# Row fetches on two helper queues, PSUM copies on VectorE, and the steps behind a pair's sums spread over six pairs

## The chip, the core and the metric

The kernel runs on one core of a Trainium2 chip. The metric is the device time of one execution in microseconds. Ten runs of the kernel before had a median of 15896.23 us (15894.68 to 15897.35).

An engine runs its own instructions in order and waits on semaphores for the others: TensorE (PE) multiplies matrices, VectorE (DVE) and ScalarE (ACT) work on elements, GpSimd (POOL) here issues gathers, SyncE (SP) issues transfers. ScalarE issues transfers too.

## The reference

One layer of a graph network with 50,000 nodes of 160 features (64 scalars and 32 vectors of three) and 1,650,000 edges, sorted by destination. Each edge takes the features of its source, mixes them with its four attributes and five small weight matrices into a message, and the messages of a destination are summed. The sum goes through two more matrices, and the result is `layernorm(x + (x + relu(h)))`.

```
ss, vv = (s[src], v[src])
e0 = sh[:, 0:1]
e1 = sh[:, 1:4]
dot = jnp.einsum('eui,ei->eu', vv, e1)
out0 = C0 * (ss * e0 @ W1 + dot * INV3 @ W2)
...
m_agg = jax.ops.segment_sum(m, dst, num_segments=n)
hs = m_agg[:, :MUL0] @ Ws * LIN_S
...
return x + jax.nn.relu(h)
...
x = _layernorm(x + _L0_gnn_ref(...), axis=-1)
```

## The kernel before

The weights commute with the sums, so the kernel first sums `attribute k times source row` over the edges of a destination, for k = 0 to 3, and applies one combined 160x(4x160) matrix afterwards (`weights` builds it as BWa and BWb).

The edges are cut into units of 128. Six units (G) are a group, whose destinations fit into a window of 32 nodes (W). Two groups are a pair (PG), four a chunk (QG), and 20 a superblock (SG) of 120 units. There are 12,894 units, 2,149 groups, 1,075 pairs, 538 chunks, 108 superblocks and 391 blocks of 128 nodes.

`load` brings a superblock's source and destination numbers (`ri`) and attributes (`ra`) with three SyncE transfers, casts the numbers on ScalarE (`rf`, line 203), makes byte offsets of rows of x from them (`ro`, line 206), and transposes everything on PE, so that an edge stands on a partition. `place` subtracts the first destination of each group (`rel`).

`group_sums` does a pair. For each unit one indirect DMA on GpSimd gathers 128 rows of x into one of eight `xg` buffers (line 236). VectorE makes a one-hot matrix of the destinations (`hot`, line 241) and multiplies it by the four attributes (`ha`, line 244). PE multiplies each unit's `ha` with its rows into `ps` (line 249), and ScalarE copies `ps` to `A` (line 255).

One unit in 60 is not gathered by GpSimd. Its rows are fetched by SyncE: `HELP` names pairs 4 and 9 of each superblock, and the last unit of such a pair is a helper unit, with a buffer `xr`. `fetch` works in four batches of 32 rows, one after each of the four pairs before: a TENSOR_LOAD brings 32 offsets into registers (line 323), then 32 transfers of one row of 640 B each follow (line 328).

When a chunk's two pairs are summed, `second` runs after the next pair's sums: `apply_weights` transposes `A` on PE into `pt` (line 267), ScalarE copies it to `at` (270), PE multiplies by BWa and BWb into `phc` (277), ScalarE copies to `hp` (281). For each node block that is now complete, `block` loads its x rows (`xt`, SyncE, line 289), doubles them on ScalarE (line 291), makes a one-hot matrix (`hot2`, 295), adds the chunks' rows with PE into `phb` (300), and calls `norm`: VectorE's relu and add (`y`, 151) and statistics (153, 155), ScalarE's square root (157), VectorE's reciprocal and scaling (158, 160), and a ScalarE store (161).

The order of instructions on each engine is chosen by a scheduler from this program. Transfers issued by SyncE and ScalarE signal their landing on eight semaphores, taken in turn by both queues together in the built order. A transfer waits, before it is issued, until the transfer eight places earlier, which used the same semaphore, has landed. Gathers on GpSimd have eight semaphores of their own.

Behind the main loop there is a second path (from line 400) for edges that don't fit the windows; it isn't taken here.

Of the kernel before, what the change touches and what calls it, by code (L numbers as in the profile page):

```python
# [30 lines left out]
F32 = mybir.dt.float32  # L31
I32 = mybir.dt.int32
U8 = mybir.dt.uint8
AF = mybir.ActivationFunctionType
ALU = mybir.AluOpType
AX = mybir.AxisListType
ET = mybir.EngineType
PSUM = bass.MemoryType.PSUM

P = 128  # L40
MUL0, MUL1 = 64, 32
D = MUL0 + 3 * MUL1
NK = 4
EPS = 1e-5
C0 = 1.0 / math.sqrt(MUL0 + MUL1)
C1 = math.sqrt(3.0 / (MUL0 + 2 * MUL1))
# [5 lines left out]
W = 32  # L52
# [4 lines left out]
HELP = {ET.SP: (4, 9)}  # L57
# [19 lines left out]
def tile_gnn_resnorm(ctx: ExitStack, tc: tile.TileContext, x, src, dst, attr, W1, W2, W3, W4, W5, Ws, Wv, out, n_edges):  # L77
# [12 lines left out]
    nc.gpsimd.memset(eps_t, EPS)  # L90
# [57 lines left out]
    def norm(pool, ph, x2, n, row):  # L148

        y = pool.tile([P, D], F32, name="y")  # L150
        nc.vector.scalar_tensor_tensor(y[:n], ph, 0.0, x2, op0=ALU.max, op1=ALU.add)  # L151
        st = pool.tile([P, 6], F32, name="st")
        nc.vector.bn_stats(st[:n], y[:n])
        mv = pool.tile([P, 2], F32, name="mv")
        nc.vector.bn_aggr(mv[:n], st[:n])  # L155
        rstd = pool.tile([P, 1], F32, name="rstd")
        nc.scalar.activation(rstd[:n], mv[:n, 1:2], AF.Sqrt, bias=eps_t[:n])  # L157
        nc.vector.reciprocal(rstd[:n], rstd[:n])  # L158
        o = pool.tile([P, D], F32, name="o")
        nc.vector.tensor_scalar(o[:n], y[:n], mv[:n, 0:1], rstd[:n], op0=ALU.subtract, op1=ALU.mult)  # L160
        nc.scalar.dma_start(out[row, :], o[:n])
# [15 lines left out]
    with tc.tile_pool(name="once", bufs=1) as once, tc.tile_pool(name="raw", bufs=2) as rawp, \  # L177
# [3 lines left out]
            tc.tile_pool(name="hp", bufs=alive + 3) as hpp, tc.tile_pool(name="node", bufs=3) as np_, \  # L181
# [8 lines left out]
        nc.vector.tensor_copy(slotsP, slots)  # L190

        def load(s):

            n = (min(NG, (s + 1) * SG) - s * SG) * G
            u0 = s * SG * G
            e = slice(u0 * P, (u0 + n) * P)
            ri = rawp.tile([P, 2, P], I32, name="ri")
            ra = rawp.tile([P, P, NK], F32, name="ra")
            nc.sync.dma_start(ri[:n, 0, :], src1[e].rearrange("(u p) o -> u (p o)", p=P))
            nc.sync.dma_start(ri[:n, 1, :], dst1[e].rearrange("(u p) o -> u (p o)", p=P))  # L200
            nc.sync.dma_start(ra[:n].rearrange("u p k -> u (p k)"), attr[e].rearrange("(u p) k -> u (p k)", p=P))
            rf = rawp.tile([P, 2, P], F32, name="rf")
            nc.scalar.copy(rf[:n], ri[:n])

            ro = rawp.tile([P, P], I32, name="ro")
            nc.scalar.mul(ro[:n], ri[:n, 0, :], 4.0 * D)
            offsets[s] = ro
            pi = psI.tile([P, 2, P], F32, name="pi")
            for i in range(2):
                nc.tensor.transpose(pi[:, i, :n], rf[:n, i, :], ident[:n, :n])  # L210
            si = idxp.tile([P, P], I32, name="si")
            nc.vector.tensor_copy(si[:, :n], pi[:, 0, :n])
            pk = psK.tile([P, NK, P], F32, name="pk")
            for k in range(NK):
                nc.tensor.transpose(pk[:, k, :n], ra[:n, :, k], ident[:n, :n])
            return s, n, si, pi, pk

        def place(loaded):

            s, n, si, pi, pk = loaded  # L220
            rel = idxp.tile([P, P], F32, name="rel")
            nc.vector.tensor_tensor(
                rel[:, :n].rearrange("p (g j) -> p g j", j=G), pi[:, 1, :n].rearrange("p (g j) -> p g j", j=G),
                baseB[:, s * SG:s * SG + n // G].unsqueeze(2).to_broadcast([P, n // G, G]), op=ALU.subtract)
            nc.vector.tensor_reduce(extremes[:, 0, s:s + 1], rel[:, :n], axis=AX.X, op=ALU.min)
            nc.vector.tensor_reduce(extremes[:, 1, s:s + 1], rel[:, :n], axis=AX.X, op=ALU.max)
            return si, rel, pk

        def group_sums(placed, u, ng, q):

            si, rel, pk = placed
            n = ng * G
            xg = rowp.tile([P, PG * G, D], F32, name="xg")
            xr = fetched.pop(q, None)
            for j in range(n - (xr is not None)):
                nc.gpsimd.indirect_dma_start(  # L236
                    out=xg[:, j, :], out_offset=None, in_=x,
                    in_offset=bass.IndirectOffsetOnAxis(ap=si[:, u + j:u + j + 1], axis=0))

# [6 lines left out]
                                    .to_broadcast([P, n, NK, W]), op=ALU.mult)  # L246
            ps = psA.tile([P, PG, D], F32, name="ps")
            for j in range(n):
                nc.tensor.matmul(ps[:, j // G, :], ha[:, j].rearrange("p k w -> p (k w)"),  # L249
                                 xr if xr is not None and j == n - 1 else xg[:, j, :],  # L250
                                 start=j % G == 0, stop=j % G == G - 1)
            for eng in HELP:
                fetch(q, eng)
            A = sump.tile([P, PG, D], F32, name="A")
            nc.scalar.copy(A[:, :ng], ps[:, :ng])  # L255
            return A, ng

        def apply_weights(pairs):
# [3 lines left out]
            for f0, f1 in ((0, P), (P, D)):  # L262
                pt = psM.tile([P, QG, P], F32, name="pt", tag="misc")
                g = 0
                for A, n in pairs:
                    for i in range(n):
                        nc.tensor.transpose(pt[:f1 - f0, g, :], A[:, i, f0:f1], ident)  # L267
                        g += 1
                at = sump.tile([f1 - f0, NK, QG, W], F32, name=f"at{f0}")
                nc.scalar.copy(at[:, :, :ng].rearrange("f k g w -> f g k w"),  # L270
                               pt[:f1 - f0, :ng].rearrange("f g (k w) -> f g k w", w=W))
                parts.append(at)
            ph = psM.tile([P, D], F32, name="phc", tag="misc")
# [7 lines left out]
            nc.scalar.copy(hp[:ng * W], ph[:ng * W])  # L281
            return hp, ng * W

        def block(b, hps):
            nb = min(P, N - b * P)
            cs = of_block[b]
            row = slice(b * P, b * P + nb)
            xt = np_.tile([P, D], F32, name="xt")
            nc.sync.dma_start(xt[:nb], x[row, :])
            x2 = np_.tile([P, D], F32, name="x2")  # L290
            nc.scalar.mul(x2[:nb], xt[:nb], 2.0)  # L291
# [4 lines left out]
                                    rr[:, :len(cs)].unsqueeze(2).to_broadcast([P, len(cs), P]), op=ALU.is_equal)  # L296
            ph = psM.tile([P, D], F32, name="phb", tag="misc")
# [3 lines left out]
            norm(np_, ph[:nb], x2[:nb], nb, row)  # L301
# [3 lines left out]
        offsets, fetched = {}, {}  # L305
        ppair = SG // PG
        steps = P // ROWS
        todo = {}
        for s in range(NSC):
            for eng, at in HELP.items():  # L310
                for m in at:
                    q = s * ppair + m
                    if q >= steps and (s * SG + (m + 1) * PG) <= NG:
                        for i in range(steps):
                            todo.setdefault((q - steps + i, eng), []).append((q, s, (m + 1) * PG * G - 1, i))

        def fetch(q, eng):

            for q1, s, u, i in todo.pop((q, eng), []):
                if i == 0:  # L320
                    fetched[q1] = farp.tile([P, D], F32, name=f"xr{list(HELP).index(eng)}")
                xr = fetched[q1]
# [8 lines left out]
        loaded = {0: load(0)}  # L331
# [16 lines left out]
        placed = {0: place(loaded.pop(0))}  # L348
        hps, pairs, ready = {}, [], []
        c = 0  # L350

        def second(c, pairs):
            hps[c] = apply_weights(pairs)
            for b in after[c]:
                block(b, hps)
            for old in [o for o in hps if o < of_block[min(nblocks - 1, (after[c] or [0])[-1])][0]]:
                del hps[old]

        g = 0
        while g < NG:  # L360
            s = g // SG
            if g % SG == 0 and s + 1 < NSC:
                loaded[s + 1] = load(s + 1)
            ng = min(PG, NG - g, (s + 1) * SG - g)
            got = group_sums(placed[s], (g - s * SG) * G, ng, s * ppair + (g - s * SG) // PG)
            if ready:
                second(*ready.pop())
            pairs.append(got)
            g += ng
            if g % QG == 0 or g == NG:  # L370
                ready.append((c, pairs))
                pairs, c = [], c + 1
            if g % SG == 0 and g < NG:
                placed[s + 1] = place(loaded.pop(s + 1))
                del placed[s]
        second(*ready.pop())


# [85 lines left out]
    with tc.tile_pool(name="edges2", bufs=2) as ep, tc.tile_pool(name="ops2", bufs=2) as op, \  # L464
# [3 lines left out]
        with tc.For_i(0, blocks, 1) as b:  # L468
# [51 lines left out]
            nc.scalar.mul(xt, xt, 2.0)  # L520
            norm(np_, ph, xt, NBLK, row)
# [33 lines left out]
```

## Time and profile before

| | before |
|---|---|
| median of 10 runs | 15896.23 us |
| the profiled execution | 15896.43 us |
| its span | 15894.3 us |
| mean granted TensorE clock | 0.676 |
| HBM traffic | 73 GB/s over the span |
| share of the 16 DMA engines' span taken by gathers (q0) | 24.6% |
| share taken by SyncE's transfers (q1) | 2.2% |

A page of the profile has the busy time of each engine, then groups of instructions: line, engine, operation, output and inputs, shape, count, then busy microseconds, mean nanoseconds of one, and the idle time of that engine just before them with what ended it. "issue" there means that the engine waited for nothing that the profile shows. A view by line gives minimum/median/maximum durations in ns. The queue in order of time gives start, length, engine, line, tiles and count, with idle time in brackets. Instructions of SyncE, and those of ScalarE that issue transfers, don't count as busy; they are shown as SPq and ACTq. The profile is even over its whole length: the busy shares of the 40 slices differ by a tenth at most.

### The profile page before, as it was taken

To read this page: it belongs to the slowest core of one execution; us is meant where nothing else is said; L and a number is where in the kernel's file an instruction comes from. 1 tells how busy PE (TensorE), PEld (TensorE's weight loads), DVE (VectorE), ACT (ScalarE), POOL (GpSimd) and SP (SyncE) were. 2 spreads that over 40 slices of the span, in tenths; PEclk is the share of its full clock that TensorE was granted. 3 is DMA by queue.
4 is the path that set the end of the run, shared out by engine and by line. 5 is a ranking of instruction groups with operands and counts; after the bars stand their busy time and mean duration, and the time that the engine had idled before them with its cause. 6 is when DMAs were issued, how large, how long until landed. Compare 5 with 4: busy or idle time off the path is not lost. (4 is left out here: it accounts for less than half of the span.)

```text
span 15894.3 us, 172106 instructions
## 1 busy us (share of the span) xinstructions
PE 8955.7 (56%) x43943; PEld 7311.8 (46%) x43944; DVE 3430.4 (22%) x5361; ACT 1480.1 (9%) x3691; POOL 11990.8 (75%) x12691
## 2 busy tenths in 40 slices
PE   5555565555555655555555555555555555555565
PEld 4444444444444444444444444444444444444454
DVE  2222222222222222222222222222222222222222
ACT  0000000000000000000000000100000000000000
POOL 7777777777777777777777777777777777777776
PEclk7666666666666666666666666666766666666666
DMA  3222222222222222222222222222222222222222
GB/s 76 74 73 74 74 73 74 74 73 74 74 74 73 74 74 73 74 75 73 74 74 75 73 74 74 74 74 74 74 74 74 73 75 74 73 74 74 73 74 69
DMA packets 823370, 1173.58 MB, mean 74 GB/s; under 512 B 250282, under 2 KB 606342, under 8 KB 822244
## 3 DMA queue, kind: packets, MB, share of 16 engines
q0 software_dynamic: 608640, 1039.56, 24.6%
q1 hardware_dynamic: 156868, 90.41, 2.2%
q10 hardware_dynamic: 56864, 32.58, 0.7%
q8 instruction: 350, 5.73, 0.1%
q14 instruction: 648, 5.31, 0.1%
HBM read 1129.30 MB, written 32.25 MB: 73 GB/s over the span
## 5 line engine op out<-in xcount | busy, mean ns | idle before, releaser
L236 POOL DMA_INDIRECT xg<-in_x,si x12680 | 11989.2, 946 | 3870.7 <-issue 3720.4
L249 PE MATMUL ps<-xg,ha 128*128 128x160 f32 x25360 | 5632.5, 365 | 1459.8 <-DMA xg<-in_x,si 1381.9
L249 PEld LDWEIGHTS ps<-xg,ha 128*128 128x128 f32 x25360 | 4348.6, 225 | 2585.2 <-DMA xg<-in_x,si 2303.9
L244 DVE TENSOR_TENSOR ha<-hot,pk 128x1536 f32<-128x1536 f32 x1075 | 1883.3, 1752 | 7937.2 <-PE ps L249 7936.9
L249 PE MATMUL ps<-xr,ha 128*128 128x160 f32 x428 | 186.1, 538 | 5114.6 <-DMA xr<-in_x 3842.4
L249 PEld LDWEIGHTS ps<-xr,ha 128*128 128x128 f32 x428 | 107.7, 312 | 5181.3 <-issue 3001.3
L151 DVE SCALAR_TENSOR_TENSOR y<-phb,x 128x160 f32<-128x160 f32 x391 | 125.1, 320 | 4291.1 <-ACT x L291 4258.7
L267 PE MATMUL pt<-ident,A 128*128 128x128 f32 (+1 forms) x4298 | 866.8, 338 | 266.8 <-DVE y L151 249.2
L277 PE MATMUL phc<-BWa,at 128*128 128x160 f32 x4304 | 939.3, 376 | 17.9 <-ACT at L270 14.4
L277 PEld LDWEIGHTS phc<-BWa,at 128*128 128x128 f32 x4304 | 832.5, 249 | 87.6 <-ACT at L270 69.5
L277 PE MATMUL phc<-BWb,at 32*128 32x160 f32 x4304 | 846.8, 342 | 0.0
L300 PE MATMUL phb<-hp,hot 128*128 128x160 f32 x4584 | 805.0, 331 | 7.3 <-ACT hp L281 7.3
L270 ACT COPY at<-pt 128x512 f32<-128x512 f32 (+1 forms) x1076 | 607.3, 579 | 1947.9 <-PE pt L267 1937.7
L277 PEld LDWEIGHTS phc<-BWb,at 32*128 32x128 f32 x4304 | 701.7, 213 | 119.5 <-issue 119.3
L267 PEld LDWEIGHTS pt<-ident,A 128*128 128x128 f32 (+1 forms) x4298 | 567.3, 146 | 410.8 <-DVE y L151 311.4
L300 PEld LDWEIGHTS phb<-hp,hot 128*128 128x128 f32 x4584 | 723.2, 211 | 61.4 <-issue 48.2
L255 ACT COPY A<-ps 128x320 f32<-128x320 f32 x1075 | 445.6, 425 | 3245.0 <-PE ps L249 3159.3
L241 DVE TENSOR_TENSOR hot<-slotsP,rel 128x384 f32<-128x384 f32 x1075 | 594.2, 553 | 30.5
L291 ACT ACTIVATE x<-xt 128x160 f32<-128x160 f32 x391 | 131.4, 336 | 4875.3 <-DMA xt<-in_x 4873.2
L295 DVE TENSOR_TENSOR hot<-slotsP,rr 128x768 f32<-128x768 f32 (+2 forms) x391 | 362.2, 926 | 4.4 <-PE phb L300 4.4
L281 ACT COPY hp<-phc 128x160 f32<-128x160 f32 x538 | 157.4, 293 | 1780.9 <-PE phc L277 1750.6
L157 ACT ACTIVATE rstd<-mv,eps_t 128x1 f32<-128x1 f32 x391 | 115.2, 295 | 1763.7 <-DVE mv L155 1759.5
(70 smaller groups left out, 1003.2 us busy)
## 6 DMA issues: line engine op xcount, KB each, us to landing
xr<-in_x SPq DMA_DIRECT2D x27392, 0.6 KB
xg<-in_x,si POOLq DMA_INDIRECT x12680
xt<-in_x SPq DMA_DIRECT2D x390, 80.0 KB
out<-o ACTq DMA_DIRECT2D x390, 80.0 KB
ra<-in_attr SPq DMA_DIRECT2D x107, 240.0 KB
ri<-in_src SPq DMA_DIRECT2D x107, 60.0 KB
ri<-in_dst SPq DMA_DIRECT2D x107, 60.0 KB
baseI<-base_d SPq DMA_DIRECT2D x1, 1076.0 KB
```

What stands on the lines that cost most here:

```text
L236: nc.gpsimd.indirect_dma_start(out=xg[:, j, :], out_offset=None, in_=x, in_offset=bass.IndirectOffsetOnAxis(ap=si[:, u + j:u + j + 1], axi ...
L241: nc.vector.tensor_tensor(hot[:, :n], slotsP[:, 0:W].unsqueeze(1).to_broadcast([P, n, W]), rel[:, u:u + n].unsqueeze(2).to_broadcast([P, n ...
L244: nc.vector.tensor_tensor(ha[:, :n], hot[:, :n].unsqueeze(2).to_broadcast([P, n, NK, W]), pk[:, :, u:u + n].rearrange("p k u -> p u k").un ...
L249: nc.tensor.matmul(ps[:, j // G, :], ha[:, j].rearrange("p k w -> p (k w)"), xr if xr is not None and j == n - 1 else xg[:, j, :], start=j ...
L255: nc.scalar.copy(A[:, :ng], ps[:, :ng])
L267: nc.tensor.transpose(pt[:f1 - f0, g, :], A[:, i, f0:f1], ident)
L270: nc.scalar.copy(at[:, :, :ng].rearrange("f k g w -> f g k w"), pt[:f1 - f0, :ng].rearrange("f g (k w) -> f g k w", w=W))
L277: nc.tensor.matmul(ph[:ng * W], at[:, k, :ng].rearrange("f g w -> f (g w)"), bw[:, k, :], start=i == 0, stop=i == 2 * NK - 1)
L281: nc.scalar.copy(hp[:ng * W], ph[:ng * W])
L291: nc.scalar.mul(x2[:nb], xt[:nb], 2.0)
L295: nc.vector.tensor_tensor(hot2[:, :len(cs)], slotsP.unsqueeze(1).to_broadcast([P, len(cs), P]), rr[:, :len(cs)].unsqueeze(2).to_broadcast( ...
L300: nc.tensor.matmul(ph[:nb], hot2[:r, i, :nb], hp[:r], start=i == 0, stop=i == len(cs) - 1)
```

## The change

- `HELP` now has periods: SyncE fetches one unit in 44 and ScalarE one in 48, in batches of 32 rows that are spread evenly over the period. The last batch is issued two pairs ahead of the pair that uses the rows. SyncE has the buffers `xr0`, ScalarE `xr1`, three of each. Helper units become 292 for SyncE and 267 for ScalarE (before: 214 for SyncE alone).
- The copies out of PSUM to `A`, `at` and `hp` go from ScalarE to VectorE.
- The combined weights and epsilon are scaled so that half of the sum is normalized: `y = relu(h)/2 + x` with epsilon/4. The doubling of x on ScalarE goes away.
- The steps behind a pair's sums become functions that a table runs after later pairs: the cast of a loaded superblock after the first pair, its transposes after the fourth; `ha` of a pair before the sums of the pair in front; `turn` one pair after the chunk, the weights and the block's loads after two, the block's sums after four, the square root after five, the store after six.
- `hp` and `node` pools get one more buffer.

```
-HELP = {ET.SP: (4, 9)}
+HELP = {ET.SP: 44, ET.Activation: 48}
...
             A = sump.tile([P, PG, D], F32, name="A")
-            nc.scalar.copy(A[:, :ng], ps[:, :ng])
+            nc.vector.tensor_copy(A[:, :ng], ps[:, :ng])
...
             hp = hpp.tile([P, D], F32, name="hp")
-            nc.scalar.copy(hp[:ng * W], ph[:ng * W])
+            nc.vector.tensor_copy(hp[:ng * W], ph[:ng * W])
...
+        for h, (eng, period) in enumerate(HELP.items()):
+            first = PG * G + h * period // 2
+            while True:
+                at = [int(first + i * period / nbatch) // (PG * G) for i in range(nbatch)]
+                q = at[-1] + 2
+                if q >= len(pairs) or pairs[q][2] < PG:
+                    break
+                s, g, ng = pairs[q]
+                u = (g - s * SG + ng) * G - 1 - len(helped.get(q, []))
+                helped.setdefault(q, []).insert(0, (eng, h))
+                for i, p in enumerate(at):
+                    batches.setdefault(p, []).append((eng, h, q, s, u, i))
+                first += period
...
+        def fetch(p):
+            for eng, h, q, s, u, i in batches.get(p, []):
                 if i == 0:
+                    fetched[q, h] = farp.tile([P, D], F32, name=f"xr{h}")
+                xr = fetched[q, h]
...
+        for p, (s, g, ng) in enumerate(pairs):
+            if p % per == 0 and s + 1 < NSC:
+                raws[s + 1] = load(s + 1)
+                after_pair(p + 1, do_cast, s + 1)
+                after_pair(p + 4, do_place, s + 1)
+            rows = gather(placed[s], (g - s * SG) * G, ng * G,
+                          [fetched.pop((p, h)) for _, h in helped.get(p, [])])
+            if p + 1 < len(pairs):
+                s1, g1, ng1 = pairs[p + 1]
+                has[p + 1] = spread(placed[s1], (g1 - s1 * SG) * G, ng1 * G)
+            sums.append(group_sums(rows, has.pop(p)))
+            fetch(p)
+            if (g + ng) % QG == 0 or g + ng == NG:
+                after_pair(p + 1, do_turn, c, sums)
+                for b in after[c]:
+                    after_pair(p + 4, do_block, b)
+                    after_pair(p + 5, do_root, b)
+                    after_pair(p + 6, do_store, b)
+                after_pair(p + 2, do_weights, c)
+                sums, c = [], c + 1
+            for f, args in later.pop(p, []):
+                f(*args)
```

`spread` is the part of `group_sums` that made `hot` and `ha`; `gather` the part with the indirect DMAs; `turn` the transposes of `apply_weights`; `nodes` the loads and one-hot matrix of `block`; `norm1`, `norm2` and `norm3` the three parts of `norm` up to the statistics, the square root, and the rest with the store. Their instructions are otherwise those shown above.

## The prediction

> **What bounds the kernel now.** I read the busy times first, then the costliest groups, then the GpSimd queue in order of time, then the queue of SyncE. All of these are views of the one profiled execution of before.
>
> ```profile
> PE 8955.7 (56%) x43943; PEld 7311.8 (46%) x43944; DVE 3430.4 (22%) x5361; ACT 1480.1 (9%) x3691; POOL 11990.8 (75%) x12691
> L236 POOL DMA_INDIRECT xg<-in_x,si x12680 | 11989.2, 946 | 3870.7 <-issue 3720.4
> L249 PE MATMUL ps<-xr,ha 128*128 128x160 f32 x428 | 186.1, 538 | 5114.6 <-DMA xr<-in_x 3842.4
> ```
>
> GpSimd looks 75% busy, but nearly all of its idle time (3720.4 of 3870.7 us) ended by itself ("issue"). The queue in order of time shows why: a gather starts every 1.25 us, whatever the other engines do.
>
> ```profile
> 8022.07 0.94 POOL L236 DMA_INDIRECT xg<-in_x,si  x1 [0.30 <-issue]
> 8023.32 0.95 POOL L236 DMA_INDIRECT xg<-in_x,si  x1 [0.30 <-issue]
> 8024.57 0.94 POOL L236 DMA_INDIRECT xg<-in_x,si  x1 [0.31 <-issue]
> ```
>
> The view of line 236 has the first start at 7.0 and the last at 15861.1 us, so the spacing is 15854.1/12,679 = 1.2504 us. Gathers fill the span: 7 us of start, 12,679 x 1.2504, and 33 us from the start of the last one. The profiled execution took 15896.43 us (its span 15894.3 and 2.1 around it), 0.2 above the median. PE waits 3842 us for helper rows (xr), yet GpSimd loses nothing by it, because eight xg buffers let it run ahead.
>
> The next lines are SyncE's and ScalarE's issue: one row of a helper unit, the load of 32 row offsets, the store, a run of helper rows, one xt, and what SyncE waited for.
>
> ```profile
> L328 SPq DMA_DIRECT2D xr<-in_x x27392: 227/228/403, 20.5 to 15837.8; - x200
> L323 SPq TENSOR_LOAD <-ro x856: 2083/2178/2443, 18.2 to 15825.1; - x172
> L161 ACTq DMA_DIRECT2D out<-o x391: 338/338/371, 179.1 to 15885.6; - x196
> ...
> 7999.88 7.65 SPq L328 DMA_DIRECT2D xr<-in_x  x24
> ...
> 8024.70 0.37 SPq L289 DMA_DIRECT2D xt<-in_x  x1
> ...
> SPq L328 <- DMA out<-o: 4483.5, 385, 67.5
> ```
>
> Twenty-four rows in 7.65 us: (7.65 - 0.228)/23 = 0.3227 us a row. The 4483.5 us tell that SyncE can be held by a store of ScalarE. All DMAs of SyncE and ScalarE take eight completion semaphores in turn, and each waits until the DMA eight places earlier has landed. Today the eight are nearly all SyncE's own.
>
> **The change, part by part.** *Gathers removed.* 292 units go to SyncE and 267 to ScalarE, 559 in place of 214, so 12,335 gathers are left of 12,680. GpSimd alone would give 7.0 + 12,334 x 1.2504 + 33.2 = 15,463, with 2 around it 15,465 us: 431 less. That is 14.35 us for each of the 1,075 pairs, and the price of any cover from here on.
>
> *SyncE's added work.* 292 units are 1,168 batches: 2.24 us for the offsets (2.18 and the step to the next instruction) and 32 x 0.3227, so 12.57 us, 14,682 in all. 390 xt at 0.43 (the row's 0.37 and the step) make 168; 321 loads of edges at about 0.45 (0.41 to 0.52 apart in the trace) 144. Sum 14,994 us against 15,424 of gathers: it fits only if a batch loses no more than 0.37 us.
>
> *What a batch loses.* In the built program the two helpers stand alternately: of SyncE's 37,376 rows, 30,116 have just four of SyncE's own DMAs among the last eight (24,285 of 27,392 had eight of eight before), and SyncE waits on semaphores 0, 2, 4, 6 while ScalarE waits on 1, 3, 5, 7. So a row waits for the row four back to land. The trace has the landing, as the last update of that semaphore: 1.414 us after the issue starts on average (26,994 rows; 5 to 95% 1.183 to 1.658), and a held row starts 0.017 later. Four issues take 4 x 0.3227 = 1.29. With eight places the landing was hidden (2.58); with four the mean of the longer of both is 1.445, 0.361 a row. The added wait isn't in the trace of before; I bound it by its rows. Low end 0 (a quarter of the landings are under 1.285). High end: the first row of a batch lands after 1.333, those in full flow after about 1.42, so one queue at work adds 0.09; a second queue may add as much again, 1.505 + 0.017, mean 0.386 a row: 30,116 x 0.064 = 1,917. I take half of that addition, 0.371 a row: 30,116 x 0.0486 = 1,464 us, since the row is nearer to the measured mean than to either end.
>
> *ScalarE's queue.* It loses the copies (445.6 + 607.3 + 157.4 busy) and x2 (131.4), and gains 1,068 batches at 12.57, 13,425 us; with 29,980 rows at the four-back wait (1,457), 391 roots (115), stores (391 x 0.40 = 156) and 108 casts (78) it comes to 15,231, some 1,230 below SyncE's 16,458: 3.1 us of slack for each root. Each root now stands in front of a batch and waits for VectorE's mv, which waits for PE. In the built order 140 of 363 roots come at most one SyncE batch behind the last rows that PE must first consume; for these, a round of PE (8955.7/1,075 = 8.3 us a pair) and 0.9 of VectorE can be exposed. 151 such roots in all x (9.2 - 3.1) = 920 us at most, 0 at least (PE's round mostly over); I take 460, as half of a round is likely done. Behind the root stand 32 rows and the store; SyncE meets them through the shared semaphores.
>
> *Moved to VectorE.* Nearest rows are its operations out of PSUM: 128x160 0.320 us (line 151), 128x384 0.553 (line 241), so 128x320 0.49, 128x512 0.69: 1,075 x 0.49 + 1,076 x 0.69 + 538 x 0.32 = 1,441 us. VectorE goes to 4,870 us, 4.5 a pair, beside a batch of 12.57; PE's 8.3 a pair hides there as well. If that cover were gone the 1,441 would count in full.
>
> *Spread over six pairs, halved weights, earlier hot2, ha and place.* No matmul or transpose is added, and x2 goes because the weights carry the half. These steps are moved on PE and VectorE, which wait for rows either way: nothing, and the reach of 0 to -131 (x2) lies beside the helper queues. The xt load is moved among SyncE's rows; it landed within 2.01 us (issued 8007.63, used 8009.64), and the next offsets load of 2.24 mostly covers it. Without that, 390 x 0.7 = 273.
>
> Sum: SyncE 14,994 + 1,464 + 460, and some 80 for the first offsets (18) and the two pairs and the tail after the last rows: 16,998, with 2 around it 17,000 us. GpSimd then waits for xg buffers, since PE stands at xr.
>
> **A rule against the change.** ScalarE's stores overlap 75 times with a helper row on SyncE, and in 73 both keep their 338 and 228 ns (the others 457, and 595 with 403), so I price no collision between the two issuers. The Trainium skill, Perfetto Trace Analysis, section DMA Instruction — HWDGE (DVE, Sync), says that the two share one descriptor generator, locked while an instruction uses it. If the whole 228 ns were locked, 71,552 rows would need 16,314 us, slower than before by that alone; the overlaps say that the lock is far shorter.
>
> **Rivals.** *The lanes don't bind* (faster, 15,465 us): the four-back wait costs under 0.37 us a batch, GpSimd keeps its 1.25 us spacing, and the change gives its 431 us. For it: a quarter of the landings come in time, SyncE's bare work fits. Against: the mean landing is beyond 1.29, and SyncE is at 97% without any wait. *ScalarE's in-order waits decide* (18,930): all 391 roots expose the round, 391 x 6.1 = 2,385 in place of 460. For it: today's 4483.5 us of SyncE behind stores; against: 223 of 363 roots have two batches or more to spare. *VectorE's copies hold GpSimd up* (16,900): 15,465 + 1,441, if each copy stopped the gathers for its length. Against: gathers run from 942 to 1143 ns, median 946, beside 3430 us of VectorE. *The helpers don't take what they should*: 559 units are in the built program, so this is out.
>
> **How the numbers follow.** The lane-limited case 0.60, its own range 16,130 (landings as measured, no exposed root: 14,994 + 1,057 + 80) to 18,190 (14,994 + 1,917 + 920 + 273 + 80, rounded); lanes not binding 0.20; the roots 0.11; VectorE 0.05; a balance within 0.2% (15,864 to 15,928) 0.04. A measurement of this kernel can tell 0.2%. Faster 0.20, same 0.04, slower 0.76. The range must reach the rival on the other side, 15,460, and ends at 18,200.
>
> **What would show it.** Right: GpSimd's idle time goes from "issue" to PE's ps; starts of rows on both queues 0.36 to 0.38 us apart inside a batch, with each fourth held; SyncE without any long rest; PE idle at xr. Wrong: gathers still 1.25 us apart to the end, or rows still 0.3227 apart (the window isn't what holds them), or the long waits all before roots (then the third case).

## The result and the profile after

The changed kernel took 19441.55 us (median of 8 runs, 19427.64 to 19459.75) against 15896.37 for the kernel before: a ratio of 1.223 (95% interval 1.222 to 1.224). The prediction had the side right and the size wrong: 17,000 us, with a range that ended at 18,200. The profiled execution has a span of 19463.3 us.

The page of the changed kernel, its engines and the groups that answer to those shown of before (busy time and mean, then the idle time before them and what ended most of it):

```profile
PE 7548.6 (39%) x43943; PEld 6895.9 (35%) x43944; DVE 4672.6 (24%) x8050; ACT 185.6 (1%) x611; POOL 11663.5 (60%) x12346
L246 POOL DMA_INDIRECT xg<-in_x,si x12335 | 11661.9, 945 | 7662.3 <-issue 3677.4
L267 PE MATMUL ps<-xr,ha 128*128 128x160 f32 x1118 | 373.5, 427 | 9070.7 <-DMA xr<-in_x 8231.3
L152 DVE SCALAR_TENSOR_TENSOR y<-phb,xt 128x160 f32<-128x160 f32 x391 | 126.4, 323 | 8887.0 <-DMA xt<-in_x 8883.5
```

GpSimd's own pauses ("issue", 0.30 us a gather) are as before, and when nothing holds it a gather still starts every 1.25 us. New are 3,985 us in which it waits for others, nearly all of it in these two waits (in total, times, longest):

```profile
POOL xg L246 <- DVE rel L235: 2747.9, 97, 42.8
POOL xg L246 <- PE ps L267: 1067.8, 272, 19.8
```

PE stands 9,071 us at helper rows. VectorE stands 8,884 us at `xt`, a tile that SyncE loads between its rows. In the kernel before, ScalarE stood at `xt` and VectorE behind it, and the gathers kept their pace all the same:

```profile
L151 DVE SCALAR_TENSOR_TENSOR y<-phb,x 128x160 f32<-128x160 f32 x391 | 125.1, 320 | 4291.1 <-ACT x L291 4258.7
L291 ACT ACTIVATE x<-xt 128x160 f32<-128x160 f32 x391 | 131.4, 336 | 4875.3 <-DMA xt<-in_x 4873.2
```

So such a wait alone tells little; what does is that GpSimd is now held. The kernel no longer runs at the pace of the gathers, but at that of the two helper queues, as the path below shows.

SyncE's queue in order of time, where 24 rows took 7.65 us before:

```profile
1016.06 12.37 SPq L362 DMA_DIRECT2D xr<-in_x  x30
1028.80 0.37 SPq L313 DMA_DIRECT2D xt<-in_x  x1
1031.50 11.19 SPq L362 DMA_DIRECT2D xr<-in_x  x30
```

Thirty rows in 12.37 us are 0.419 us a row. Over the whole trace the mean step inside a batch is 0.420 on SyncE and 0.417 on ScalarE. The same microseconds on the other engines, lines left out between:

```profile
1025.81 5.97 ACTq L362 DMA_DIRECT2D xr<-in_x  x15
...
1030.13 0.87 PE L267 MATMUL ps<-xr,ha 128*128 128x160 f32 x2 [44.16 <-DMA xr<-in_x]
...
1030.60 0.33 DVE L152 SCALAR_TENSOR_TENSOR y<-phb,xt 128x160 f32<-128x160 f32 x1 [42.46 <-DMA xt<-in_x]
...
1032.27 0.29 ACT L161 ACTIVATE rstd<-mv,eps_t 128x1 f32<-128x1 f32 x1 [68.30 <-DVE mv L156]
...
1034.62 1.14 ACTq L362 DMA_DIRECT2D xr<-in_x  x3
...
1039.74 0.35 DVE L167 TENSOR_SCALAR o<-y,mv,rstd 128x160 f32<-128x160 f32 x1
...
1040.13 0.38 ACTq L168 DMA_DIRECT2D out<-o  x1
1040.61 2.27 ACTq L362 DMA_DIRECT2D xr<-in_x  x5
```

This is a ring. SyncE's last rows and `xt` (1028.80) let PE and VectorE go on after 44 and 42 us of standing. VectorE makes `y`, then in its own order the copies and `ha` that had piled up, and only at 1039.74 `o`. ScalarE issued its last row at about 1035.5, and then stood until 1040.13 for the store of that `o`; its next rows, for which PE will stand again, could only follow behind.

To see how much of the time is ring and how much is rows, I followed the path back from an instruction of PE near the end: each instruction to that of its dependencies which ended last, by the semaphores of the built program and the starts, ends and landings of the trace. "Rows" are issues, landings and offset loads of both queues. Of the changed kernel, e1 and f1 the first 0.1 to 0.4 ms, where gathers set the path, are left out.

```
share of the path, %         rows SyncE  rows ScalarE   PE   VectorE  stores   xt   gathers
before                           0.2         0          0.2     0       0       0     99.5
changed kernel                  24.0        54.6       12.6    4.2     2.4     1.9     0
SyncE alone (e1)                78.8         0          6.9    6.2     4.0     3.1     0
SyncE alone, early xt (f1)      65.3         0         26.4    3.5     3.0     0.6     0
both, ring open (h2n)            7.6        90.3        0.2     0      1.0     0.1     0
SyncE alone, ring open (h1)       0          0           0      0       0       0    100
```

In the changed kernel 21% of the path is not rows but the ring's other members. Behind its first 0.4 ms gathers are on none of it.

### The profile page after: what moved, and what is told of

Its sections match the earlier page's. It is cut to its first block, busy times and chain, and to the rows that moved or that the text cites. A ratio compares the mean times of both kernels' runs of the same rounds, so it can differ in the third digit from the quotient of the medians.

```text
span 19463.3 us, 260704 instructions
## 1 busy us (share of the span) xinstructions
PE 7548.6 (39%) x43943; PEld 6895.9 (35%) x43944; DVE 4672.6 (24%) x8050; ACT 185.6 (1%) x611; POOL 11663.5 (60%) x12346
## 5 line engine op out<-in xcount | busy, mean ns | idle before, releaser
L246 POOL DMA_INDIRECT xg<-in_x,si x12335 | 11661.9, 945 | 7662.3 <-issue 3677.4
L267 PE MATMUL ps<-xg,ha 128*128 128x160 f32 x24670 | 4183.5, 331 | 147.4 <-DVE A L271 84.5
L267 PEld LDWEIGHTS ps<-xg,ha 128*128 128x128 f32 x24670 | 3942.2, 216 | 310.6 <-DVE A L271 142.6
L267 PE MATMUL ps<-xr,ha 128*128 128x160 f32 x1118 | 373.5, 427 | 9070.7 <-DMA xr<-in_x 8231.3
L267 PEld LDWEIGHTS ps<-xr,ha 128*128 128x128 f32 x1118 | 236.4, 256 | 9159.2 <-DMA xr<-in_x 5955.8
L152 DVE SCALAR_TENSOR_TENSOR y<-phb,xt 128x160 f32<-128x160 f32 x391 | 126.4, 323 | 8887.0 <-DMA xt<-in_x 8883.5
L271 DVE COPY A<-ps 128x320 f32<-128x320 f32 x1075 | 509.5, 485 | 2708.6 <-PE ps L267 2705.4
L286 DVE COPY at<-pt 128x512 f32<-128x512 f32 (+1 forms) x1076 | 706.1, 679 | 503.2 <-PE pt L283 488.8
L327 PE MATMUL phb<-hp,hot 128*128 128x160 f32 x4584 | 690.8, 301 | 0.3 <-DVE at L286 0.3
L301 DVE COPY hp<-phc 128x160 f32<-128x160 f32 x538 | 174.4, 324 | 1333.5 <-PE phc L297 1299.7
```

Of the source, the lines that this page charges most:

```text
L246: nc.gpsimd.indirect_dma_start(out=xg[:, j, :], out_offset=None, in_=x, in_offset=bass.IndirectOffsetOnAxis(ap=placed[0][:, u + j:u + j + ...
L271: nc.vector.tensor_copy(A[:, :ng], ps[:, :ng])
L286: nc.vector.tensor_copy(at[:, :, :ng].rearrange("f k g w -> f g k w"), pt[:f1 - f0, :ng].rearrange("f g (k w) -> f g k w", w=W))
L301: nc.vector.tensor_copy(hp[:ng * W], ph[:ng * W])
L327: nc.tensor.matmul(ph[:nb], hot2[:r, i, :nb], hp[:r], start=i == 0, stop=i == len(cs) - 1)
```

## The experiments

### One helper alone

```
-HELP = {ET.SP: 44, ET.Activation: 48}
+HELP = {ET.SP: 44}                       # e1; e2 has ET.Activation: 48 alone
```

> The changed kernel with SyncE alone as helper (one unit in 44, ScalarE none; 292 units, 12,602 gathers left), so that 34,262 of SyncE's 37,376 rows have eight of eight own rows in the window of semaphores. Theory (two queues in one window and the longer landing cost the time): rows 0.323 us apart again, landing 1.41 us, SyncE 14,994 us of work fits under the gathers, so 7 + 12,601 x 1.2504 + 35 = 15,798 us. Rival (the copies on VectorE, or the steps spread over six pairs, hold things up): the 1,390 us of copies or more would still be there, 16,500 us and above.

> The changed kernel with ScalarE alone as helper (one unit in 48, SyncE none; 267 units, 12,627 gathers left). Theory of the shared window: rows 0.32 to 0.33 us apart, gathers decide, 7 + 12,626 x 1.2504 + 35 = 15,830 us; the roots, stores and casts in ScalarE's queue (0.35 ms of work and some waits) fit into the 1.7 ms left. Rival (ScalarE's in-order waits for VectorE, PE and the edge loads decide by themselves): its 13,774 us of work plus 391 waits of 6 us or more, 16,200 us and above, with PE standing at xr.

Measured: e1 16511.08 us (ratio 1.0386, 1.0369 to 1.0404), e2 17301.61 (1.0882, 1.0864 to 1.0900). Both were expected near 15,800, so a window of eight does not make the loss go away. Rows were back at 0.3227 us (median of SyncE's steps 0.323) and the landing at 1.41 us, as expected, but SyncE now waited for something else. The waits of SyncE's queue in e1 (in total, times, longest):

```profile
SPq L362 <- DMA out<-o: 1127.7, 346, 43.5
```

SyncE has 15,260 us of its own work in e1, which would fit under 15,798 us of gathers; with these waits it does not. In the built program `xt` stands just ahead of the store that needs it, and the row that takes the store's semaphore stands eight of SyncE's DMAs behind `xt`, so SyncE has only those eight to issue while VectorE and ScalarE make the store. In e2 it is ScalarE's rows that stand some 2,740 us behind SyncE's `xt` and `ra`.

### Both helpers, thinner

```
+HELP = {ET.SP: 60, ET.Activation: 64}
```

> The changed kernel with both helpers, but one unit in 60 (SyncE) and one in 64 (ScalarE): 414 units, 12,480 gathers left. Theory (the two queues together have a rate that they cannot exceed, 66.7 us for each SyncE unit in the changed kernel): 214 SyncE units take 14,270 us, below the gathers, so the gathers decide and the time is 7 + 12,479 x 1.2504 + 35 = 15,646 us, faster than both kernels. Rival (the waits are of the roots, stores and casts, whose number does not fall with the units): 3,500 us over the gathers shrinks little, 17,000 us and above.

Measured: 15674.25 us, ratio 0.9859 (0.9843 to 0.9876), 28 us over the expectation. The group of gathers in e3:

```profile
L246 POOL DMA_INDIRECT xg<-in_x,si x12480 | 11799.6, 945 | 3812.6 <-issue 3705.0
```

All but 108 us of the idle time is the gathers' own. Two helpers, copies on VectorE and the spread steps are together faster than the kernel before, as long as the queues have slack.

### Trying to open the ring

e4 and e5b move the roots and stores six pairs later and the edge loads four pairs earlier (e4 with both helpers, e5b with SyncE alone); e6b leaves out 801 of ScalarE's offset loads, and so sums wrong rows.

```
-                    after_pair(p + 5, do_root, b)
-                    after_pair(p + 6, do_store, b)
+                    after_pair(p + 11, do_root, b)
+                    after_pair(p + 12, do_store, b)
...
+            if p % per == 6 and s + 2 < NSC:
+                raws[s + 2] = load(s + 2)
...
+                if i == 0 or eng != ET.Activation:      # e6b alone
```

> The changed kernel with the edge loads four pairs earlier and the roots and stores six pairs later (node buffers 8 in place of 4); rows, units and window as they were. If ScalarE's in-order waits (1,154 us before casts, 998 before stores, and through them 1,778 us of SyncE behind ScalarE's rows) are what my sum lacked: 19,442 less 1,800 to 2,200, near 17,400 us. If it is the rows' own window and landing (2,228 us on SyncE, 2,552 on ScalarE): 19,000 to 19,500 us.

> The same kernel as e5_sp_alone_later, again, because in that session the kernel before took 24,977 us instead of 15,897. Theory (a late store of ScalarE, eight places before, holds SyncE's rows): without the 1,123 us behind stores the gathers decide, 7 + 12,601 x 1.2504 + 35 = 15,798 us. Rival (SyncE's rate or VectorE's steps bound the run): 16,300 to 16,500 us.

> The same kernel as e6_act_loads, again for the same reason: the changed kernel without 801 of ScalarE's 1,068 offset loads (the first 32 rows of a unit are fetched four times). Theory (the helpers move in step): near 17,800 us. Rival (SyncE's own rows fill its queue): 19,200 to 19,450 us.

Measured: e4 19477.46 us (1.2251, 1.2230 to 1.2271), e5b 16791.74 (1.0561, 1.0543 to 1.0578), e6b 20389.28 (1.2824, 1.2802 to 1.2845). All three missed. e4 and e5b did not do what I meant: the scheduler puts a root or a store where its inputs are ready, not where the table calls it, and in e5b's built program the row on the store's semaphore still stood 8 to 13 DMAs behind what the store needs (SyncE waited 1,417 us behind stores). So neither kernel says anything for or against the ring. In e6b less work of ScalarE made the kernel slower: its waits before casts, for edge loads that SyncE issues between its rows, grew from 1,165 us to 3,147, and those before roots from some 390 to some 2,050. Nothing in it shows that SyncE had paid for ScalarE's offset loads; why the sum grew by 948 us I did not settle.

Next `xt` was fetched earlier, with its one-hot matrix, by three chunks (f1 SyncE alone, f2 both as in the change, f5 both thinner).

```
+LEAD = 3
...
-            for b in after[c]:
-                of_nodes[b] = nodes(b)
+            for c2 in [c + LEAD] if c else range(LEAD + 1):
+                for b in after[c2] if c2 < NCH else []:
+                    of_nodes[b] = nodes(b)
```

> SyncE alone as helper (one unit in 44, 12,602 gathers), with the residual's tile xt fetched six pairs earlier (node buffers 8). In the run with SyncE alone the path that set the end ran from SyncE's rows to xt, to VectorE's y and o, to ScalarE's store, and back to a row of SyncE that waits for the store's semaphore; the built program put that row 8 DMAs behind xt, and here it stands 14 to 35 behind the last DMA that the store needs. Theory (xt, fetched too late in SyncE's order, closes this ring): the 1,123 us behind stores go and the gathers decide, 7 + 12,601 x 1.2504 + 35 = 15,798 us. Rival (SyncE's rows themselves are too slow for one unit in 44): 16,300 to 16,500 us.

> The changed kernel with xt fetched six pairs earlier (node buffers 8), nothing else changed. On the path that set its end, rows and offsets of the two helpers make 79%, and PE, VectorE, stores and xt 21%, some 4,100 us of 19,463. Theory (this part is there because xt comes late and roots and stores behind it hold ScalarE's rows): it goes, and what is left is SyncE's own work with the four-back wait, 14,994 + 2,228 + 230 = 17,450 us. Rival (the rows of both helpers in one window, with landings of 1.53 and 1.58 us, set the pace whatever the nodes do): 19,000 us and above.

> The same with one unit in 54 (SyncE) and one in 58 (ScalarE), 12,435 gathers left. If xt was the hold, SyncE's 238 units at 17,450/292 = 59.8 us take 14,230, and the gathers decide: 7 + 12,434 x 1.2504 + 35 = 15,590 us. If the rows in one window set the pace at 66.7 us a unit: 15,875 us.

Measured: f1 18075.84 us (1.1370, 1.1351 to 1.1389), f2 19484.79 (1.2253, 1.2232 to 1.2273), f5 16615.51 (1.0455, 1.0437 to 1.0472). VectorE no longer stood at `xt`, and nothing was gained. SyncE's waits in f1:

```profile
SPq L363 <- DMA out<-o: 2694.3, 378, 69.3
```

The ring had another way to close. In the built program of f1 the row on a store's semaphore stood 14 or 15 DMAs behind what the store needs for nearly every store (the expectation had 14 to 35), which is some 5 us of issue and at times an offset load; but the store also waits until PE has caught up with the pairs that piled up while it stood at `xr`, and the path of f1 has 26% of PE for 7% in e1. So, by the path, an early tile does not help when the store itself is still too close.

### The ring opened

In h1 SyncE alone helps; `o` is made as before, but its store is issued eight pairs later, by SyncE, behind a row of that pair. In h2n both help as in the change: the root runs after nine pairs, `o` is made after 14, and the store goes out after 18; root and store each stand behind a row of ScalarE. `xt` is early in both, the edge loads in h1 only, and the nodes' tiles have more buffers. No work is left out.

```
+        def do_send(b, rows):
+            o, nb, row = outs.pop(b)
+            if rows:
+                with tc.issue_after(rows.pop().ins):
+                    nc.sync.dma_start(out[row, :], o[:nb])   # h2n: nc.scalar
...
-                    after_pair(p + 5, do_root, b)         # h2n alone
-                    after_pair(p + 6, do_store, b)
+                    after_pair(p + 9, do_root, b)
+                    after_pair(p + 14, do_store, b)
+                    after_pair(p + 18, do_send, b, marks) # h1: p + 14
```

> SyncE alone as helper (one unit in 44, 12,602 gathers), xt fetched six pairs earlier, edge loads four pairs earlier, and the stores issued by SyncE itself, eight pairs after their o is made and behind a row of that pair, so that in the built program some 500 SyncE DMAs lie between what a store needs and the store. Fetching xt early alone gave 18,076 us, with 2,689 us of SyncE behind stores and PE making 26% of the path. Theory (rows wait for a store, the store for VectorE, PE and so for the rows themselves; nothing else holds SyncE): the ring is open, the gathers decide, 7 + 12,601 x 1.2504 + 35 = 15,798 us. Rival (SyncE's own issue is too slow for one unit in 44): 16,300 us and above.

> The changed kernel (one unit in 44 and one in 48) with xt fetched six pairs earlier, roots four pairs later, o eight pairs later and the stores twelve pairs later, each behind a row of ScalarE of its pair. The order of rows and semaphores is as before (30,103 SyncE rows have four of eight own). Theory A (the ring through roots, xt and stores makes the 21% of the path that are not rows): the ring is open and what is left is SyncE's own work with the four-back wait, 14,994 + 2,228 + 230 = 17,450 us or somewhat more. Theory B (the rows of two queues in one window keep this pace by themselves): 19,000 us and above.

> The same with one unit in 54 (SyncE) and one in 58 (ScalarE), 12,435 gathers. By theory A SyncE's 238 units at 59.8 us take 14,230 and the gathers decide: 7 + 12,434 x 1.2504 + 35 = 15,590 us, below the 15,674 of one in 60 and 64. By theory B (66.7 us a unit): 15,875 us or more.

Measured: h1 15801.45 us, ratio 0.9939 (0.9922 to 0.9955), where 15,798 was expected. The ring is what held the kernel with one helper: some 500 DMAs now lie between what a store needs and the store, and no row waits behind a store. The store changed its queue and its distance together, so which of the two would have been enough is not shown. The page of h1, gathers and helper units:

```profile
L250 POOL DMA_INDIRECT xg<-in_x,si x12602 | 11916.2, 946 | 3848.9 <-issue 3601.4
...
L271 PE MATMUL ps<-xr,ha 128*128 128x160 f32 x584 | 199.1, 437 | 0.0
```

h2n took 18356.40 us (1.1545, 1.1526 to 1.1564), between the two theories: 1,085 us below the change, and 906 above theory A. Its path is 98% rows. PE still stands at `xr`, and the waits of its engines and of SyncE's queue are now:

```profile
PE ps L271 <- DMA xr<-in_x: 9379.0, 270, 46.6
```

```profile
SPq L364 <- DMA xr<-in_x: 2335.1, 7946, 3.0
SPq L364 <- DMA out<-o: 93.9, 125, 7.5
```

For comparison, SyncE's waits in the changed kernel:

```profile
SPq L362 <- DMA xr<-in_x: 3524.3, 7334, 24.9
```

The longest wait for a row fell from 24.9 us to 3.0: no more long rests, only many short ones. What is left is the window and the landing. Steps of rows and landings, from the starts and the last update of each row's semaphore in the trace of the change:

```
SyncE rows with 4 of the last 8 DMAs its own   30042   mean step 0.404 us, 60% start within 0.06 of a landing
SyncE rows with 8 of 8 its own                  2870   mean step 0.331 us,  0%
landing of a SyncE row, no ScalarE row within 1 us             1.31 us
landing of a SyncE row, 4 or 5 ScalarE rows within 1 us        1.65 to 1.68 us
landing of a ScalarE row, no SyncE row / 4 or 5 within 1 us    1.41 / 1.66 to 1.70 us
```

Four rows back and a landing of 1.66 to 1.70 us make (1.68 + 0.017)/4 = 0.424 us a row; ScalarE's steps in h2n have a mean of 0.421. With that step ScalarE's queue is full: 14,328 us of rows, 2,395 of offset loads, 1,311 for casts and their waits, some 290 of roots and stores.

The count of rows nearby is in part a result of the landing, since quick landings let more rows be issued: with six rows of the other queue within 1 us the landing is 1.44 us (SyncE, 1,884 rows) and 1.47 (ScalarE, 3,155). Means over all rows are free of this: 1.41 us in e1 and 1.40 in e2, with one queue; 1.53 and 1.57 (SyncE, ScalarE) in the change, 1.57 and 1.61 in h2n. Window and landing both count. SyncE's rows of the change with four of eight own have a step of 0.383 us when no ScalarE row is within 1 us (3,175 rows), and of 0.420 with four or more (19,938), against 0.331 with eight of eight. And 38 rows of ScalarE had eight of eight own and four or more SyncE rows around them: they landed after 1.68 us and stood 0.336 apart. They are few; no run gave two queues at work a window of eight each throughout.

h3n is the kernel of h2n with one unit in 54 and one in 58:

```
+HELP = {ET.SP: 54, ET.Activation: 58}
```

It took 15621.92 us, ratio 0.9825 (0.9809 to 0.9842): the fastest of all, 52 us faster than e3 and 32 us over the expectation. At the same density f5, with the ring closed, took 16,616. Its page:

```profile
L250 POOL DMA_INDIRECT xg<-in_x,si x12435 | 11758.3, 946 | 3800.5 <-issue 3604.2
...
L271 PE MATMUL ps<-xr,ha 128*128 128x160 f32 x918 | 312.2, 438 | 148.2 <-DMA xr<-in_x 143.2
```

### Runs in sessions where the kernel before took 24,980 us

Six runs fell in sessions whose own runs of the kernel before took 24,977 to 24,981 us. e5 and e6 (repeated above as e5b and e6b), e8 (the change with 54 and 58), e9 (ScalarE issues everything), and h4 twice (h3n with 50 and 56).

> SyncE alone as helper (one unit in 44, 12,602 gathers), and the roots and stores six pairs later, the edge loads four pairs earlier (node buffers 8). With SyncE alone the run gave 16,511 us: SyncE stood 1,123 us behind stores of ScalarE that were not yet written, and its bare work is 15,260. Theory (the row waits for whatever DMA stood eight places before it, on either queue, and a store that is itself late holds it): with the stores later the 1,123 go, SyncE fits under the gathers, 7 + 12,601 x 1.2504 + 35 = 15,798 us. Rival (SyncE's rate or the steps on VectorE bound the run): 16,300 to 16,500 us.

> The changed kernel, but ScalarE loads offsets only for the first of a unit's four batches and fetches the same 32 rows four times; this leaves out 801 of ScalarE's 1,068 offset loads, and nothing of SyncE's queue. Theory (the two helpers move in step, because each waits for semaphores of the other's rows, so SyncE pays for ScalarE's offset loads as well, some 1.5 us for each of its own batches): SyncE saves up to 801 x 2.2, the time is near 17,800 us. Rival (SyncE's own rows and their longer landing fill its queue): SyncE's work is the same, 19,200 to 19,450 us.

> The changed kernel with one unit in 54 (SyncE) and one in 58 (ScalarE), 12,433 or so gathers left. Theory (66.7 us for each SyncE unit is what the pair of queues needs when nothing else holds them): 238 units need 15,875 us and the gathers 15,590, so it is at the edge, 15,590 to 15,900 us, and the best period lies between this and one in 60 (15,674). Rival (the queues' need falls with fewer units, since the waits fall too): 15,590 us.

> ScalarE alone as helper (one unit in 48, 12,627 gathers), and the edge loads and the residual's tiles issued by ScalarE too, so that SyncE issues nothing in the main part. With SyncE issuing those the run gave 17,302 us, and ScalarE's rows stood 2,738 us behind DMAs of SyncE. Theory (a row waits for a late DMA of the other queue): these waits go, ScalarE's 14,100 us of work fit under the gathers, near 15,830 us. Rival (ScalarE's in-order waits for VectorE, PE and the loads hold it as long): 17,000 us and above.

> The kernel of h3n_mid with one unit in 50 (SyncE) and one in 56 (ScalarE), 12,408 gathers left. In h2n_both, with the ring open, ScalarE needed 18,356/267 = 68.7 us for a unit, and SyncE by its own steps some 60. If that is the rate of the queues, 56 units of gathers (70.0 us) and 50 (62.5 us) just leave room and the gathers decide: 7 + 12,407 x 1.2504 + 35 = 15,556 us. If the two in step need more than that: 15,700 us and above.

> The same kernel as h4_dense, again, because in that session the kernel before took 24,979 us instead of 15,897. The rate with the ring open (68.7 us for a ScalarE unit, some 60 for a SyncE unit) leaves room below 70.0 and 62.5: 15,556 us. If the two in step need more: 15,700 us and above.

Measured against those: e5 27225.34 us (ratio 1.0898, 1.0883 to 1.0914), e6 29848.27 (1.1952, 1.1935 to 1.1969), e8 26683.20 (1.0685, 1.0670 to 1.0700), e9 26643.14 (1.0668, 1.0653 to 1.0683), h4 25828.01 (1.0343, 1.0329 to 1.0357) and 25857.89 (1.0350, 1.0336 to 1.0365). Their queues lose time that the others don't (last section), so no theory is judged by them. It stays open whether 50 and 56 would be faster than h3n, and whether ScalarE alone reaches the gathers' time.

## Why the prediction was wrong, step by step

- *GpSimd bound the kernel before, at 1.2504 us a gather.* Right: h1, h3n and e3 end within 32 us of 7 + gathers x 1.2504 + 35.
- *Copies to VectorE (1,441 us), weights, spreading: hidden.* Right. The copies took 1,390 us and VectorE 4,673 (4,870 predicted), and kernels that have them all run at the gathers' pace. The rival in which VectorE's copies hold GpSimd is out.
- *SyncE's work, 14,994 us without waits.* Right in kind: e1 showed 15,260 with start and tail.
- *The four-back wait, 0.371 a row.* The mechanism was right: a row waits for the row four back to land, and steps stand at 0.404 with four of eight own beside 0.331 with eight of eight. The size was wrong, and this is the term that failed most. I took the landing from one queue at work (1.414 us), and allowed a second queue half, at most the whole, of the 0.09 us that one queue adds to itself. Where both are in full flow it adds 0.25 to 0.37, so the landing is 1.65 to 1.70. On ScalarE rows cost 14,328 us where my sum had 13,425 - 2,392 + 1,457 = 12,490: 1,838 more. The high end of that bound (0.386 a row) was too low as well. This term alone would not have left the range: it puts SyncE's queue at 16,998 + 30,116 x (0.404 - 0.371) = 17,992 us and ScalarE's at 15,231 + 1,838 = 17,069. The rest is the next two steps.
- *ScalarE's queue, 15,231, some 1,230 below SyncE's.* Wrong: the sum went by the other queue. With the ring open ScalarE's queue sets the end at 18,356. Besides the rows it lacked the waits before the casts (1,176 us in h2n, 1,165 in the change), which I had priced at nothing beyond 78 us for the casts: the edge loads stand in SyncE's queue between rows and come late. That these add in full isn't shown: in e4 the waits for edge loads fell to some 610 us and the time did not, in another order of rows; there ScalarE stood 1,181 us behind rows of SyncE (1 us in the change) and 774 before roots.
- *In-order waits before roots, 460 us.* For the roots alone about right: ScalarE stood 394 us before them in the change (111 in h2n). But it was too narrow in kind. ScalarE also stood 1,022 us before its stores, until VectorE had made `o` (17 in h2n); for these I had priced the issue, 156 us, and no wait. Together with `xt` and the shared semaphores they close the ring, and opening it (with `xt` early) is worth 19,442 - 18,356 = 1,085 us. I bounded roots alone, at 920. The rival in which ScalarE's in-order waits decide (18,930) had this mechanism, but the larger part of the miss is rows and casts.
- Together: 15,231 + 1,838 + (1,176 + 135 - 78) for casts is 18,302, and with 1,085 for the ring 19,387 of 19,442. This is an account and not a further test: ScalarE's queue has no rest in h2n, so its parts must add up to that kernel's time, and 1,085 is the difference of two measured times.
- *xt at nothing, 273 if uncovered.* Fetching it early by itself gained nothing (f2, 19,485 us). That doesn't make the price right: `xt` and its landing are 1.9% of the path of the change, some 370 us, as a member of the ring, and I had named no cover for it there.
- *What would show it.* SyncE without long rests: wrong, 289 waits over 1 us behind ScalarE's rows made 1,397 us in the change (41 and 53 us in h2n). Rows 0.36 to 0.38 apart: wrong, 0.42. PE idle at `xr`: right. GpSimd's new idle time was to end at PE's `ps`; 1,068 us did, but 2,748 ended at VectorE's `rel`, the superblock that is placed late because its edge loads are late: in e4, with the edge loads four pairs earlier, no such wait is left, and those for PE's `ps` are 3,996.
- *The skill's rule.* The Trainium skill, Perfetto Trace Analysis, section DMA Instruction — HWDGE (DVE, Sync), has one descriptor generator behind both queues. The rows say how little that costs the issue: the medians are 228 ns on SyncE and 234 on ScalarE (228 in e1 and 235 in e2, with one queue), and in a tenth of the stretches of 40 rows in which both are at work a row comes each 0.216 us or faster, which a lock of all 228 would not allow. The same page says that a DMA's bar in the profile leaves out the moving of the data. That is where the cost was: landings grew while the bars stayed the same.

## What to carry to other kernels

When two queues take completion semaphores in turn, price a row by the landing that it waits for, and take that landing from a stretch in which both queues are at work: here it was a sixth to a fifth longer (1.65 to 1.70 us) than in a trace of one queue (1.41), and the window half as long. Where a queue that feeds the kernel also carries something made at the kernel's end (a store, a root), look in the built order how many transfers lie between what it needs and the one that waits for it; calling it later in the program does not move it, and if the distance is short, the feeding queue waits for its own product. A helper should get less than its queue can carry: 559 helper units cost 22%, 459 with the ring open gained 1.75%, and 414 with nothing else changed gained 1.4%.

## What the runs showed of the hardware that was not expected

A row of 640 B, issued in 228 ns either way, lands 1.31 us after its issue when the other queue is silent for 1 us around it, and 1.65 to 1.68 us after when that queue issues four or five rows there (the change, SyncE's rows; 1.44 with six). What in the path of a transfer takes the longer time was not tried.

The same kernel (e5 and e5b) took 27,225 us in one session and 16,792 in another, with the kernel before at 24,977 and 15,897. A gather took 946 ns and a VectorE copy (`A`) 491 ns (medians) in both. But SyncE's register moves, all of 29 ns in the one, took 0.65 to 0.75 us in some 4,000 of 37,380 cases in the other, and the step from a row's issue to the next move, 264 ns in the median of both, was 0.7 or 1.4 us in a sixth of them. By these rows it is the flow of instructions that slowed, not the work; what slowed it was not tried.
